# A 7x7 depthwise convolution on TensorE: from row bands to tiles of six by four pixels

## The chip, the cores and the metric

The kernel runs on one core of one Trainium2 chip. The metric is the device time of one execution in microseconds (us), median of the runs. A core has five engines that run side by side, each taking its own instructions in order: TensorE (PE; its weight loads are listed as PEld), VectorE (DVE), ScalarE (ACT), GpSimd (POOL) and SyncE (SP), whose queue here issues nearly all DMAs.

## The reference

Two attention layers on x of 4 images, 256 channels, 64 x 64 pixels, all in float32. Cut to what matters here, the second layer is:

```python
qkv = conv1x1(x, w_qkv, b_qkv)                 # 768 channels: q, k, v of 8 heads of 32
attn = softmax(q @ k.T * 32 ** -0.5)           # within each of 4 areas of 16 image rows
out = attn @ v
out = out + dwconv7(v, w_pe, b_pe)             # each channel its own 7x7 filter, padding 3
x = x + conv1x1(out, w_proj, b_proj)
```

The input of each layer is group-normalised. The first layer is attention of all 4096 pixels to 1024 keys that 2x2 convolutions with step 2 make. The change touches dwconv7 and what stands around it.

## The kernel before, in words

**Units.** The work is 128 units: batch by batch the first layer (A0 to A3), then the second (B0 to B3), 16 units each. A unit is 512 query pixels (a "chunk" of 8 image rows) and 128 channels (4 heads); it goes through 8 steps of 128 keys. In a step TensorE makes the scores of 4 heads (L261, tile s), ACT the exponentials (L265, tile p), TensorE the weighted sums (L272, tile av), and DVE adds up p (L797) for the divisors. The loop over steps at the end of the function writes all engines' orders out by hand: nothing is reordered later, so an engine whose next instruction waits keeps all behind it waiting.

**The plan.** All other work is put into this loop. `at(g, j, f)` has f emitted at unit g, step j; `task(n, f)` puts a generator into a side queue, of which one to three parts go on TensorE in each step. So projections, the convolution and their loads have fixed places among the steps of attention, and the places are the same constants before and after.

**v and the convolution.** `plan_values(b, c, start)` loads a chunk of the first layer's result (hv), normalises it on ACT (L243), makes v by matmuls (vals_ps) and copies it with its bias to the tile vout (L669), with zero columns at the sides (L658, L659). vout is stored twice: by four DMAs into vala for the attention of the second layer (L677), and by eight, one for each image row, into vals, the image with its rows in reverse order (L682). The starts are set so that batch 0 has 3.4 units per chunk, batch 1 1.0, batch 2 1.6 (the two overlap from unit 48 on) and batch 3 0.4 (units 66 to 70).

From unit 70.5, every 0.52 units, `plan_conv(n)` handles four channels of all batches. It loads from vals, for the upper and the lower half of the image, 42 rows three times, each time shifted by one column, so that 126 partitions hold (shift, row) (L705, tile rows). The 7x7 filter stands in a band matrix, loaded for 8 channels at a time (L717, tile band). For each channel and half three matmuls accumulate, for the columns 0, 3 and 6 of the filter and their neighbours (L732): 126 x 32 weights, 32 output rows, 4 batches x 64 columns = 256 moving columns. Four matmuls with 32 output partitions each stand side by side in the array. ACT copies the result (L739), and two DMAs store it in conv, channel by batch by pixel (L741).

`load_rest` reads a chunk back from conv by one DMA (L556, tile cv), `add_conv` adds the attention and the bias on DVE (L572), `project` multiplies by w_proj (tile ops), adds the residual (L583) and stores (L586). For batches 0 to 2 this runs from unit 105.3, one chunk each 0.8 units; for batch 3 beside its own attention.

**DMAs.** The SP queue issues all of these in the order of the plan. Each of its DMAs uses one of eight semaphores in rotation and so waits for the landing of the one eight before it.

Of the kernel before, what the change touches and what calls it, by code (L numbers as in the profile page):

```python
# [32 lines left out]
XP = WW + 8  # L33
BAND = HH // 2 + 2 * HALO
BROWS = 42
TC = 8
NTAP = 49
# [17 lines left out]
def direct_path(  # L55
# [32 lines left out]

    vals = dram.tile([HH + 2 * HALO + BROWS - BAND, C, B, XP], FP, name="vals")

    vala = [[dram.tile([4, HD, NH, 4, XP], FP, name=f"vala_{b}_{a}") for a in range(NAREA)] for b in range(B)]
    conv = dram.tile([C, B, N], FP, name="conv")

    bands = dram.tile([C // TC, 9, BROWS + HH // 2 - 1, TC], FP, name="bands")

# [368 lines left out]
    def plan_b(b, u):  # L464
# [13 lines left out]
        def make_k(a, qd, half):  # L478
            if qd == 0 and half == 0:
                kvs["k"] = k_tile(("B", b, a))  # L480
            k, ps = kvs["k"], ps_side(f"k1ps_{b}_{a}_{qd}_{half}")
            for t in range(CT):
                product(
                    ps, lhsT=wqkv_sb[:, t, 1, qd * P : (qd + 1) * P],
                    rhs=hs[a][:, t, half * CH : (half + 1) * CH], start=(t == 0), stop=(t == CT - 1),
                )
                if t == 0:
                    yield

            S.activation(  # L490
                k[:, qd, :].rearrange("p (j t i) -> p t j i", t=4, i=32)[:, 2 * half : 2 * half + 2],
                ps.rearrange("p (t j i) -> p t j i", t=2, i=32), AF.Identity, bias=bqkv_sb[:, 1, qd : qd + 1],
            )
            if qd == 1 and half == 1:
                ks["B", b, a] = k

        def load_v(a, half):
            vcs[a, half] = pool.tile([P, NH // 2, 4, XP], FP, tag="vc", name=f"vc_{b}_{a}_{half}", bufs=2)
            nc.sync.dma_start(
                vcs[a, half], vala[b][a][:, :, half * NH // 2 : (half + 1) * NH // 2].rearrange("t c h r x -> (t c) h r x")  # L500
            )

        def make_v(a, half):

            if half == 0:
                kvs["v"] = v_tile(("B", b, a))
            v, vc = kvs["v"], vcs.pop((a, half))
            V.transpose(
                out=v[:, :, half * P : (half + 1) * P].rearrange("p (r j) (h c) -> p h r j c", j=2, c=HD),
                in_=vc[:, :, :, HALO : HALO + WW].rearrange("p h r (j w) -> p h r j w", w=HD),  # L510
            )
            if half == 1:
                vs["B", b, a] = v
# [40 lines left out]
        def load_rest(c):  # L554
            cv = chunk_tile(f"cv_{b}_{c}")
            nc.sync.dma_start(cv, conv[:, b, c * CH : (c + 1) * CH].rearrange("(t p) n -> p t n", p=P))  # L556
            att = None
# [5 lines left out]
            rest[c] = cv, att  # L563

        def add_conv(c):
            cv, att = rest[c]
# [4 lines left out]
            for t in range(CT):  # L571
                V.scalar_tensor_tensor(cv[:, t, :], cv[:, t, :], bpe_sb[:, t : t + 1], att[:, t, :], ALU.add, ALU.add)  # L572

        def project(c, to):
# [7 lines left out]
            xm = made_x[c]  # L582
            V.scalar_tensor_tensor(xm[:, to, :], ps, bproj_sb[:, to : to + 1], xm[:, to, :], ALU.add, ALU.add)  # L583
            if to == 1:
# [29 lines left out]


    def plan_zeros(g):


        def zeros():
            zero = pool.tile([P, 8 * B * XP], FP, tag="rows", name="zero", bufs=2)  # L620
            V.memset(zero, 0.0)
            for lo, hi in ((0, 3), (67, 71), (71, 74)):
                nc.sync.dma_start(
                    vals[lo:hi].rearrange("r c b x -> (r c b x)").rearrange("(p n) -> p n", n=8 * B * XP),
                    zero[: (hi - lo) * C // 8],
                )
            flat = bands.rearrange("k x i c -> (k x i c)").rearrange("(p n) -> p n", p=P)
            nc.sync.dma_start(flat, zero[:, : flat.shape[1]])

        def taps():  # L630
            tap = pool.tile([NTAP, C], FP, tag="cout", name="tap", bufs=2)
            nc.sync.dma_start(tap, wpe.rearrange("c k -> k c"))
            for n in range(7):
                nc.sync.dma_start(
                    bands[:, :7, BAND - 1 - n, :].rearrange("k x c -> x k c"),
                    tap[7 * n : 7 * n + 7, :].rearrange("x (k c) -> x k c", c=TC),
                )
# [6 lines left out]
    def plan_values(b, c, start):  # L644
# [10 lines left out]
        def values(t):  # L655
            if t == 0:
                vout = made["v"] = pool.tile([P, CT, RC, XP], FP, tag="rows", name=f"vout_{b}_{c}", bufs=2)
                V.memset(vout[:, :, :, :HALO], 0.0)  # L658
                V.memset(vout[:, :, :, HALO + WW :], 0.0)  # L659
            h, vout = made["h"], made["v"]  # L660
            ps = ps_side(f"vals_ps_{b}_{c}_{t}")
            for tt in range(CT):
# [6 lines left out]
            S.activation(  # L669
                vout[:, t, :, HALO : HALO + WW], ps.rearrange("p (r w) -> p r w", w=WW), AF.Identity,  # L670
                bias=bqkv_sb[:, 2, t : t + 1],
            )
            if t == CT - 1:
                stored[b, c] = True
                for n in range(2):
                    for tt in range(CT):
                        nc.sync.dma_start(  # L677
                            vala[b][c // 2][2 * (c % 2) + n, :, 4 * tt : 4 * tt + 4].rearrange("c h r x -> h c (r x)"),
                            vout[:, tt, 4 * n : 4 * n + 4, :].rearrange("p r x -> p (r x)"),
                        )  # L680
                for r in range(RC):
                    nc.sync.dma_start(  # L682
                        vals[HALO + HH - 1 - c * RC - r, :, b, :].rearrange("(t p) x -> p t x", p=P), vout[:, :, r, :]
                    )

# [6 lines left out]

    band_tiles = {}

    def plan_conv(n, start):

        made = {}

        def load():
            row, size = C * B * XP, 4 * B * XP  # L700
            need(stored, (B - 1, NCH - 1))
            made["x"] = xs = pool.tile([3 * BROWS, 2, 4, B, XP], FP, tag="rows", name=f"rows_{n}", bufs=2)
            for half in range(2):
                for s in range(3):
                    nc.sync.dma_start(  # L705
                        xs[s * BROWS : (s + 1) * BROWS, half].rearrange("p c b x -> p (c b x)")[:, : size - s],
                        bass.AP(
                            tensor=vals.tensor, offset=vals.offset + (1 - half) * (HH // 2) * row + n * size + s,
                            ap=[[row, BROWS], [1, size - s]],
                        ),  # L710
                    )
            k, part = divmod(4 * n, TC)
            if part == 0:
                band = band_tiles[k] = pool.tile([3 * BROWS, 3, HH // 2, TC], FP, tag="band", name=f"band_{k}", bufs=2)
                step = (BROWS + HH // 2 - 1) * TC
                for s in range(3):
                    nc.sync.dma_start(  # L717
                        band[s * BROWS : (s + 1) * BROWS].rearrange("p g y c -> p g (y c)"),
                        bass.AP(
                            tensor=bands.tensor, offset=bands.offset + (9 * k + s) * step,  # L720
                            ap=[[TC, BROWS], [3 * step, 3], [1, HH // 2 * TC]],
                        ),
                    )

        def convolve():
            xs, (k, part) = made.pop("x"), divmod(4 * n, TC)
            ps = ps_side(f"conv_ps_{n}").rearrange("p (i b x) -> p i b x", i=2, b=B)
            for i in range(2):
                for g in range(3):
                    for m in range(4):  # L730
                        c = 2 * (m // 2) + i
                        T.matmul(  # L732
                            ps[HD * m : HD * m + HD, i], lhsT=band_tiles[k][:, g, :, part + c],
                            rhs=xs[:, m % 2, c, :, 3 * g : 3 * g + WW], start=(g == 0), stop=(g == 2),
                        )
                    if (i, g) in ((0, 1), (1, 0)):
                        yield
            out = pool.tile([P, 2 * B, WW], FP, tag="cout", name=f"cout_{n}", bufs=2)
            S.copy(out, ps.rearrange("p i b x -> p (i b) x"))  # L739
            for ch in range(2):  # L740
                nc.sync.dma_start(  # L741
                    conv[4 * n + 2 * ch : 4 * n + 2 * ch + 2].rearrange("i b (y x) -> y (i b) x", x=WW),
                    out[HH * ch : HH * (ch + 1)],
                )

        when = int(start * NKT)
        at(0, when, load)
        at(0, when + 4, lambda: task(3, convolve))


# [693 lines left out]
```

## Time and profile before

| | |
|---|---|
| median of 3 runs (lowest, highest) | 3271.41 us (3269.73, 3272.02) |
| profiled execution: its time, its span | 3270.47 us, 3268.7 us |
| TensorE clock granted | 0.997 |
| DMA packets, bytes, mean rate | 319853, 397.27 MB, 122 GB/s |
| under 512 B | 182652 packets |
| convolution, first to last matmul | 1797.9 to 2653.2 us |
| stores into vals, first to last issue | 542.6 to 1786.0 us |
| reads of conv, first to last issue | 2657.6 to 3211.8 us |

The span runs from the first to the last instruction; the profiled execution has its own time, which stands 0.9 us under the median. "Busy" is the time in which an engine has an instruction in work; a group is all instructions of one line, operation and tile. DMA issues of SP are listed with the time that the queue took to issue them, not to move the data.

### The profile page before, as it was taken

What the parts mean: (1) busy time and instruction counts of PE and PEld (TensorE: products, weight loads), DVE (VectorE), ACT (ScalarE), POOL (GpSimd) and SP (SyncE); (2) the same over time, 40 slices, a digit from 0 to 9 for tenths busy, and PEclk for the clock granted to TensorE, in tenths of its full rate; (3) what the DMA queues carried; (4) which work ended last, traced back from release to release, by engine and by line L of the source; (5) the groups of instructions that cost most, each with busy time, mean ns of one, the idle gap of its engine ahead of it and who ended that gap; (6) DMA issues with size and microseconds to landing.
All of it is one profiled execution on the core that took longest, in us unless ns stands there. A gap on an engine that the chain in (4) does not pass through costs nothing.

```text
span 3268.7 us, 72561 instructions
## 1 busy us (share of the span) xinstructions
PE 3218.2 (98%) x29730; PEld 961.1 (29%) x29730; DVE 2491.6 (76%) x2621; ACT 2525.6 (77%) x2993; POOL 487.2 (15%) x923
## 2 busy tenths in 40 slices
PE   7999999999999999999999999999999999999997
PEld 4233323333233322222222333333333322222221
DVE  3777897779877787778876767666776778888887
ACT  3888788887888888888887777777777787776765
POOL 0111121111211111111111111111111111111111
PEclk9999999999999999999999999999999999999999
DMA  5312212313322213553236667676766643445431
GB/s 179 80 64 73 77 66 90 100 59 116 100 69 84 65 63 91 148 138 113 82 120 158 162 151 178 159 174 141 180 171 153 172 142 123 166 147 172 155 121 57
DMA packets 319853, 397.27 MB, mean 122 GB/s; under 512 B 182652, under 2 KB 215708, under 8 KB 319192
## 3 DMA queue, kind: packets, MB, share of 16 engines
q1 hardware_dynamic: 291064, 356.06, 38.5%
q0 software_dynamic: 28448, 36.48, 4.2%
q8 instruction: 236, 3.87, 0.5%
q14 instruction: 105, 0.86, 0.1%
HBM read 285.98 MB, written 106.42 MB: 120 GB/s over the span
## 4 chain that ended last, share of the span: by engine, by line
PE 94%; DMA 2%; issue 1%; ACT 1%; DVE 1%; SPq 0%; POOL 0%; DVEq 0%; ACTq 0%; POOLq 0%
PE s L261 33%; PE av L272 29%; PE conv_ps L732 5%; PE den L281 4%; PE k0ps L155 3%; PE k1ps L155 3%; PE q1ps L155 3%; PE v0ps L155 3%; PE q0ps L155 3%; PE ops L155 3%; PE vals_ps L155 3%; ACT p L265 1%; DVE p L797 1%; DMA conv<-cout 0%; DMA rows<-vals 0%
## 5 line engine op out<-in xcount | busy, mean ns | idle before, releaser
L797 DVE TENSOR_TENSOR p<-p 128x1024 f32<-128x1024 f32 x1792 | 2113.3, 1219 | 623.1 <-ACT p L265 583.3
L265 ACT ACTIVATE p<-s 128x1024 f32<-128x1024 f32 x2048 | 2016.9, 1027 | 571.9 <-PE s L261 564.0
L261 PE MATMUL s<-q,k_A 32*128 32x512 f32 x4096 | 608.2, 640 | 1.4 <-ACT p L265 0.9
L261 PE MATMUL s<-q,k_B 32*128 32x512 f32 x4096 | 588.7, 640 | 1.1 <-ACT p L265 0.8
L272 PE MATMUL av<-p,v_A 128*32 128x512 f32 x4096 | 551.1, 603 | 0.0
L272 PE MATMUL av<-p,v_B 128*32 128x512 f32 x4096 | 546.0, 604 | 0.0
L308 POOL DMA_DIRECT2D rb<-recs x508 | 252.4, 502 | 454.1 <-DMA recs<-few 377.5
L306 POOL DMA_DIRECT2D recs<-few x127 | 70.2, 553 | 1423.2 <-DVE sums L305 1372.1
L261 PEld LDWEIGHTS s<-q,k_A 32*128 32x128 f32 x4096 | 176.3, 183 | 357.8 <-issue 273.3
L261 PEld LDWEIGHTS s<-q,k_B 32*128 32x128 f32 x4096 | 162.5, 182 | 363.3 <-issue 290.5
L272 PEld LDWEIGHTS av<-p,v_A 128*32 128x32 f32 x4096 | 89.4, 108 | 383.0 <-issue 335.0
L272 PEld LDWEIGHTS av<-p,v_B 128*32 128x32 f32 x4096 | 87.6, 108 | 378.8 <-issue 332.9
L732 PE MATMUL conv_ps<-rows,band 126*32 126x256 f32 x3072 | 195.1, 379 | 0.0
L732 PEld LDWEIGHTS conv_ps<-rows,band 126*32 126x32 f32 x3072 | 123.0, 139 | 113.0 <-issue 78.3
L297 POOL DMA_DIRECT2D rows<-den_sb x127 | 74.6, 587 | 433.3 <-ACT den_sb L290 424.1
L281 PE MATMUL den<-p,ones 128*32 128x512 f32 x1024 | 137.8, 605 | 0.4 <-DVE p L797 0.4
L155 PE MATMUL ops<-cv,wp_sb 128*32 128x512 f32 x1024 | 129.8, 600 | 6.0 <-issue 6.0
L155 PE MATMUL vals_ps<-hv,wqkv_sb 128*32 128x512 f32 x1024 | 130.1, 596 | 3.9 <-ACT vout L669 3.8
L155 PE MATMUL k0ps<-taps,wk_sb 128*32 128x256 f32 x2048 | 130.6, 383 | 3.0 <-ACT taps L243 3.0
L155 PE MATMUL k1ps<-h,wqkv_sb 128*32 128x512 f32 x1024 | 128.7, 593 | 2.4 <-ACT cout L739 1.6
L155 PE MATMUL q0ps<-hq,wq_sb 128*32 128x512 f32 x1024 | 129.8, 592 | 0.0
L155 PE MATMUL q1ps<-h,wqkv_sb 128*32 128x512 f32 x1024 | 129.7, 596 | 0.1
(87 smaller groups left out, 1594.9 us busy)
## 6 DMA issues: line engine op xcount, KB each, us to landing
rb<-recs POOLq DMA_DIRECT2D x508, 64.0 KB, 2.4
rows<-vals SPq DMA_DIRECT2D x128, 189.0 KB
rows<-vals SPq DMA_DIRECT2D x128, 188.8 KB
rows<-vals SPq DMA_DIRECT2D x128, 188.7 KB
vala<-vout SPq DMA_DIRECT2D x128, 144.0 KB
vals<-vout SPq DMA_DIRECT2D x256, 72.0 KB
vc<-vala SPq DMA_DIRECT2D x32, 576.0 KB
hq<-in_x SPq DMA_DIRECT2D x32, 512.0 KB
```

What stands on the lines that cost most here:

```text
L155: T.matmul(out[cols, :], lhsT=lhsT[:, cols], rhs=rhs, start=start, stop=stop)
L261: T.matmul(pairs[h // 2][:, h % 2, :], lhsT=k[rows, unit[0], j * P : (j + 1) * P], rhs=q[rows, :], start=True, stop=True,)
L265: exps = [lambda i=i: S.activation(p[i], pairs[i], AF.Exp, scale=SCALE) for i in range(2)]
L272: T.matmul(av[HD * h : HD * h + HD, :], lhsT=v[:, j, unit[0] * P + HD * h : unit[0] * P + HD * h + HD], rhs=p[h // 2][:, h % 2, :], start= ...
L281: T.matmul(dens[g][HD * h : HD * h + HD, :], lhsT=ones, rhs=p[h // 2][:, h % 2, :], start=True, stop=True,)
L297: G.dma_start(rows, den_sb[0:P:HD, :])
L306: G.dma_start(recs.rearrange("h (q n) -> (h q) n", n=CH // HD), few[:, 1, :])
L308: G.dma_start(rb[HD * h : HD * h + HD, :], recs[h : h + 1, :].to_broadcast([HD, CH]))
L732: T.matmul(ps[HD * m : HD * m + HD, i], lhsT=band_tiles[k][:, g, :, part + c], rhs=xs[:, m % 2, c, :, 3 * g : 3 * g + WW], start=(g == 0), ...
L797: soon(1, lambda i=i: V.tensor_add(ps[0][i], ps[0][i], ps[j][i]))
```

## The change

The image is cut into tiles of 6 rows by 4 columns (11 tiles down, the last row of tiles partly empty; 16 across). One output tile of one channel depends on 12 x 10 = 120 pixels of v. These 120 pixels stand in the partitions, the 24 outputs (in an array strip of 32 with 8 rows more that aren't used) in the weights' columns, and the tiles of all batches are the moving columns: one matmul, without accumulation, makes the convolution for 6 (or 5) rows of tiles x 4 batches x 16 tiles.

So that a partition's run in HBM is contiguous, vals is laid out by every fourth pixel of a row: row, column modulo 4, channel, batch, column divided by 4. vala is laid out by every fourth pixel too, and k, v and the results are reordered to go with it. conv becomes channel, pixel in the tile, tile row, batch, tile column.

- vals is stored by 32 DMAs per chunk (8 rows x 2 channel halves x 2), with runs of 18 values.
- The filter table is filled by 49 DMAs, one for each tap, in place of 7, and loaded for 16 channels by 10 DMAs in place of 8 by 3.
- rows is loaded for four channels in two halves (6 and 5 rows of tiles), four DMAs each, three halves ahead; the pool of rows and vout tiles has three buffers in place of two.
- There are 4 matmuls and one copy for each half; each half is stored by one DMA.
- conv is read back by 16 DMAs per chunk (8 rows x 2 channel halves), with runs of 16 values; cv is then ordered by column modulo 4, and the additions on DVE read and write it in that order.
- The copy of k with its bias is made in two halves.

```diff
@@ vals, conv
-    vals = dram.tile([HH + 2 * HALO + BROWS - BAND, C, B, XP], FP, name="vals")
+    vals = dram.tile([TY * NY + 2 * HALO, TX, C, B, XT], FP, name="vals")
-    conv = dram.tile([C, B, N], FP, name="conv")
+    conv = dram.tile([C, HD, NY, B, WW // TX], FP, name="conv")
@@ plan_values: stores of a chunk
                 for r in range(RC):
-                    nc.sync.dma_start(
-                        vals[HALO + HH - 1 - c * RC - r, :, b, :].rearrange("(t p) x -> p t x", p=P), vout[:, :, r, :]
-                    )
+                    for t in range(CT):
+                        row, out = vals[HALO + HH - 1 - c * RC - r, :, t * P : (t + 1) * P, b, :], vout[:, t, r]
+                        nc.sync.dma_start(row[:3].rearrange("f p x -> p f x"), out[:, 1:])
+                        nc.sync.dma_start(row[3], out.rearrange("p f x -> p (f x)")[:, 1 : 1 + XT])
@@ taps
-            for n in range(7):
+            for n in range(NTAP):
                 nc.sync.dma_start(
...
@@ plan_conv: rows
-            for half in range(2):
-                for s in range(3):
-                    nc.sync.dma_start(
-                        xs[s * BROWS : (s + 1) * BROWS, half].rearrange("p c b x -> p (c b x)")[:, : size - s],
...
+        for a, f, fs in ((0, 0, 4), (1, 0, 4), (2, 0, 1), (2, 1, 1)):
+            p = 12 * (4 * a + f)
+            nc.sync.dma_start(
+                xs[p : p + 12 * fs].rearrange("p y c b x -> p y (c b x)")[:, : hi - lo, : size - 2],
...
@@ convolve
-            for i in range(2):
-                for g in range(3):
-                    for m in range(4):
-                        c = 2 * (m // 2) + i
-                        T.matmul(
-                            ps[HD * m : HD * m + HD, i], lhsT=band_tiles[k][:, g, :, part + c],
-                            rhs=xs[:, m % 2, c, :, 3 * g : 3 * g + WW], start=(g == 0), stop=(g == 2),
-                        )
+        for m in range(4):
+            T.matmul(
+                ps[HD * m : HD * m + HD].rearrange("p (y b x) -> p y b x", b=B, x=WW // TX),
+                lhsT=band_tiles[k].rearrange("p y (x c) -> p (y x) c", c=TC)[:, :, part + m],
+                rhs=xs[:, : hi - lo, m, :, : WW // TX], start=True, stop=True,
+            )
@@ load_rest
-            nc.sync.dma_start(cv, conv[:, b, c * CH : (c + 1) * CH].rearrange("(t p) n -> p t n", p=P))
+            for y in range(c * RC, (c + 1) * RC):
+                n, r = divmod(HH - 1 - y, TY)
+                r = TY - 1 - r
+                for t in range(CT):
+                    nc.sync.dma_start(
+                        cv[:, t, :].rearrange("p (f r x) -> p r f x", f=TX, r=RC)[:, y - c * RC],
+                        conv[t * P : (t + 1) * P, r * TX : (r + 1) * TX, n, b, :],
+                    )
@@ add_conv, project
+                V.scalar_tensor_tensor(
+                    by_column(cv[:, t, :]), by_column(cv[:, t, :]), bpe_sb[:, t : t + 1],
+                    att[:, t, :].rearrange("p (q f) -> p q f", f=TX), ALU.add, ALU.add,
+                )
...
+            x_to = xm[:, to, :].rearrange("p (q f) -> p q f", f=TX)
+            V.scalar_tensor_tensor(x_to, by_column(ps), bproj_sb[:, to : to + 1], x_to, ALU.add, ALU.add)
```

## The prediction

> **What bounds the kernel now.** I read the busy table first, then the chain that ended last, then the groups, then 100 us stretches.
>
> ```profile
> PE 3218.2 (98%) x29730; PEld 961.1 (29%) x29730; DVE 2491.6 (76%) x2621; ACT 2525.6 (77%) x2993; POOL 487.2 (15%) x923
> ...
> PE 94%; DMA 2%; issue 1%; ACT 1%; DVE 1%; SPq 0%; POOL 0%; DVEq 0%; ACTq 0%; POOLq 0%
> ...
> L732 PE MATMUL conv_ps<-rows,band 126*32 126x256 f32 x3072 | 195.1, 379 | 0.0
> ...
> L155 PE MATMUL k0ps<-taps,wk_sb 128*32 128x256 f32 x2048 | 130.6, 383 | 3.0 <-ACT taps L243 3.0
> ```
>
> TensorE is busy 98% and makes 94% of the chain, so time taken off it anywhere comes off the span, as long as nothing else ends later; the convolution is 195.1 us of it. The stretches show where:
>
> ```profile
> 1400.00:1500.00 100.00, 100.00 (x816) 25.32 (x812) 78.58 (x88) 86.74 (x105) 15.91 (x30) 1.00 0.51 142
> ...
> 1900.00:2000.00 100.00, 99.77 (x1020) 34.05 (x1016) 69.49 (x68) 74.53 (x87) 14.09 (x27) 1.00 0.68 164
> ...
> 2800.00:2900.00 100.00, 100.00 (x832) 25.19 (x828) 83.66 (x91) 73.42 (x83) 14.76 (x28) 1.00 0.44 150
> ```
>
> (Columns: PE, PEld, DVE, ACT, POOL busy, clock, DMA share, GB/s.) Three stages matter: the values stages (stores of v, up to 1786 us), the convolution (1798 to 2653) and the projections after it. TensorE is full in all three. So each stall that the change brings in one of them is added in full, and only the middle one gets shorter.
>
> The queue that is nowhere in that table is SP's, which issues every load and store of activations, in order. Its timeline at the end of the values stage (start, duration, line, DMA), and then the view of the tensor vals (least, median and longest issue in ns; who waited for it, us and times):
>
> ```profile
> 1762.09 3.15 SPq L677 DMA_DIRECT2D vala<-vout  x4
> 1765.28 8.69 SPq L682 DMA_DIRECT2D vals<-vout  x8
> 1774.02 1.22 SPq L471 DMA_DIRECT2D h<-xmid  x2
> 1775.36 3.80 SPq L677 DMA_DIRECT2D vala<-vout  x4
> 1779.20 7.14 SPq L682 DMA_DIRECT2D vals<-vout  x8
> 1786.38 1.01 SPq L705 DMA_DIRECT2D rows<-vals  x1
> ```
>
> ```profile
> L705 SPq DMA_DIRECT2D rows<-vals x384: 306/384/1669, 1786.4 to 2635.2; - x192
> L682 SPq DMA_DIRECT2D vals<-vout x256: 359/615/2145, 542.6 to 1786.0; - x128
> ...
>   PEld conv_ps L732: 0.3, 1
> ```
>
> The stores of one chunk of v (4 vala, 8 vals) take 11 us of SP back to back (1775.36 to 1786.34), the last chunk's end at 1786.3, the first rows load follows at once, and the first convolution matmul starts at 1797.9 with one wait of 0.3 us for its rows: no slack here. TensorE takes its instructions in order, so attention stands behind a late first convolution.
>
> [...] 126 rows 379 ns, 128 rows 383 ns, both 256 columns. [...] each vala store (outermost 4) brings 5 semaphore updates[...], and vala stores land 1.6 us apart, vals 0.34. [...] In this trace's packet records a 288 B packet takes 23.6 ns on average and a 256 B one 20.2, against 97.7 for 2 KB[...]. [...] the conv weights at a 32 B step: 139 ns per load against 110.
>
> **The change, part by part.**
>
> *Matmuls.* Four columns of tiles at a time, the moving columns per four channels fall from 2 x 3 x 256 = 1536 to 384 + 320 = 704, weights stay 32 wide. 195.1 x 704/1536 = 89.4 us: **105.7 us off TensorE**, all in the convolution stage. Weight loads (123 us for 3072, 1024 of them after, so 41 us, possibly more at the 64 B step) lie under the matmuls before them; uncovered they would cost that. Runs of 16 elements in the moving operand: unseen; I take 0 (high end 10 us). In that stage ACT goes from 75 to about 89% and DVE from 70 to 80% of a unit 12% shorter; neither becomes the bound.
>
> *Stores of v.* Per chunk 32 vals stores replace 8; vala is unchanged. SP: 32 chunks x 24 = 768 more DMAs. Each DMA waits for the one eight before it (eight semaphores in rotation); 8 in flight at the 2.3 us from issue to landing of the last vals store is no bound. Price of an issue: the present form (256 runs) took 467 to 470 ns back to back when nothing blocked it; a simple one (rows) 384. The two new forms are 384 and 128 runs; I take 0.47 and 0.385, with 0.04 between: 0.467 us each. The first eight stores still stand behind vala's four engines, as now: 10.5 us (median of the back-to-back chunks), less 1.3 for a shorter tail of 8 stores ahead (8 x 0.34 against about 8 x 0.18). Then 24 x 0.467 = 11.2. **20.4 us of SP per chunk** against 10.5. Packets of 72 B: between 13 ns (128 B in the trace) and 24; a pair of stores puts 34 on an engine, 0.4 to 0.8 us, under its 0.93 us of issue. Engine time doesn't bind.
>
> Where chunks come faster than that, SP falls behind. Two places, from the times of the vout copies:
> - Batches 1 and 2 overlap: chunks 10 to 19 are ready from 1301 to 1435. SP needs 10 x 20.4 + 16 other DMAs x 0.45 = 211 us, ends at 1512 instead of 1451.3: 61 us behind. Queued behind are loads that ACT normalises: hv issued at 1355.1 and used at 1362.1, hq at 1356.9 and 1374.6, hv at 1381.4 and 1393.3; after 4 to 5 us of landing they have 3, 13 and 7 us, say 9 with a few us of buffering. **Stall 52 us**: ACT waits in order, exps behind it, TensorE behind them.
> - Batch 3: eight chunks from 1680.8. 8 x 20.4 + 9 x 0.45 = 167, end at 1848 instead of 1786.3. **Stall 62 us**, at the first convolution or earlier through the three vout buffers, not twice.
> Single chunks elsewhere lag by 5 to 8 us, within slack: 0.
>
> *Rows, bands, taps.* Per four channels 8 + 2.5 + 2 DMAs instead of 6 + 1.5 + 2, some 5.5 of 13 us of SP: hidden under the other channels' matmuls, since loads go out three half-steps ahead; without that lead each half would wait some 4 us for its rows (landing median 4.7 us now). Taps: 42 more DMAs x 0.40 = 17 us of SP at about 153 us, before the first xc; that has about 13 us before its add and DVE has slack: 5 us.
>
> *Reading conv back.* Per chunk 16 DMAs of 512 runs (64 B) for one: 16 x 0.6 = 9.6 us more SP. Chunks were loaded about 27 us before their add (issued 2855.35, added 2882.5), so mostly hidden; xm, vc and h loads queue behind. 0 to 30, I take 10 us.
>
> *Strided operands.* k copy in two halves: some 0.2 us x 64 = 13 us on ACT, under its 20% of idle time: 0, 13 us if ACT were the bound. Column-order adds (L572, L583) 744 and 749 ns x 128: nothing, up to double; doubled they add 96 us to a DVE that idles about 90 us between 2690 and 3255. I take 0, high end 40.
>
> *Sum*, against the profiled 3270.5 us (span 3268.7): -105.7 + 52 + 62 + 5 + 10 = +23, 3294. The median of the runs is 0.9 above: **3295 us**.
>
> **Rivals.**
> - *SP is cheaper, and it is faster.* At S us per chunk the two stalls are (10S + 7 - 150 - 9) + (8S + 4 - 105.5); with the other 15 us they equal the 105.7 saved at S = 19.1, that is 0.41 us per short store. The shortest rows issues took 0.306; at 0.30 S is 16.4 and the time 3271 + 18 x (16.4 - 19.1) = 3222. For: those short issues. Against: they came after waits; back to back it was 0.384.
> - *The buffers absorb the lag*, and nearly all of TensorE's saving is seen: 3180. For: three vout buffers for two, DVE and ACT idle 20%. Against: the 0.3 us wait at the first convolution, TensorE in order.
> - *Short stores block one another*: each takes the 0.727 us that the stores of batch 3 average now. S = 10.5 - 1.3 + 24 x 0.77 = 27.7, 3271 + 18 x 8.6 = 3426. For: single stores up to 2.1 us. Against: those stood behind vala.
> - *DVE bounds the projections* (strided adds doubled): 3295 + 40 = 3335.
>
> **How the numbers follow.** Forecast 0.43 (own range 3255 to 3340), cheaper SP 0.27, absorbed 0.08, blocking 0.13, DVE 0.09. About 0.2% is what a measurement of this kernel tells from no change. Faster 0.27 + 0.08 and 0.01 of the forecast's low edge: 0.36; same 0.04; slower 0.60. The range 3205 to 3400 takes in the cheaper SP and the DVE case, and leaves out the absorbed one and most of the blocking one.
>
> **What would show it.** conv_ps matmuls near 89 us; vals stores x1024, SP taking about 20 us for a chunk back to back; the last vals store some 60 us later relative to the last vout copy; TensorE under 90% busy in the two values stretches, waits of ACT on hv or hq, and one of tens of us before the first conv_ps. Wrong if SP needs under 19 us per chunk, if the waits fall on idle time, or if the projections lose TensorE time.

## The result and the profile after

| | before | after |
|---|---|---|
| median of four runs (lowest, highest) | 3270.57 us (3268.65, 3272.02) | 3642.54 us (3641.67, 3648.39) |
| ratio, with its 95% interval | | 1.114 (1.112 to 1.116) |
| profiled span | 3268.7 us | 3640.9 us |
| span less TensorE's busy time | 50.5 us | 408.0 us |
| TensorE clock granted | 0.997 | 0.944 |
| DMA packets; of these under 512 B | 319853; 182652 | 815227; 613515 |

The change costs 372 us. Slower was the forecast, but by 24 us. The page of the profile after:

```profile
PE 3232.9 (89%) x27682; PEld 891.0 (24%) x27682; DVE 2511.6 (69%) x2621; ACT 2547.6 (70%) x3121; POOL 489.4 (13%) x923
...
PEclk9999999999999997878998799999999999999999
DMA  4122223233323134445424488787887775766662
...
PE 62%; DMA 17%; SPq 10%; issue 5%; DVE 3%; ACT 3%; POOL 0%; DVEq 0%; ACTq 0%; POOLq 0%
...
L757 PE MATMUL conv_ps<-rows,band 120*32 120x384 f32 (+1 forms) x1024 | 110.3, 503 | 126.9 <-DMA band<-bands 60.7
```

TensorE had 94% of the chain and has 62%. DMA and SP's queue, which were 2% and 0%, have 27%. The clock row has dips to 7 and 8 in the slices where TensorE is least busy. The convolution's matmuls are cheaper (110.3 us for 195.1), and 126.9 us of idle time now stand before them, where there was none. The stretches (PE, PEld, DVE, ACT, POOL busy, clock, DMA share, GB/s):

```profile
1400.00:1500.00 100.00, 48.20 (x348) 11.14 (x344) 31.96 (x37) 37.79 (x47) 6.85 (x13) 0.73 0.41 74
1500.00:1600.00 100.00, 63.15 (x468) 15.11 (x460) 42.84 (x49) 47.06 (x57) 7.95 (x15) 0.80 0.45 80
2230.00:2330.00 100.00, 90.64 (x756) 24.07 (x752) 68.86 (x68) 76.06 (x97) 14.19 (x27) 0.96 0.78 179
3100.00:3200.00 100.00, 99.40 (x824) 24.90 (x816) 87.76 (x90) 73.29 (x86) 14.79 (x28) 1.00 0.68 151
```

In the first two, the overlap of batches 1 and 2, no engine is full: TensorE 48 and 63%, ACT and DVE under 50%, the DMA engines 41 and 45%. What works is the queue that has no column here. SP's timeline has one of batch 3's chunks, its 4 vala and 32 vals stores (start, duration, line, DMA):

```profile
1991.56 2.60 SPq L699 DMA_DIRECT2D vala<-vout  x4
1994.20 0.55 SPq L707 DMA_DIRECT2D vals<-vout  x1
...
1999.12 0.39 SPq L707 DMA_DIRECT2D vals<-vout  x1
2000.94 0.32 SPq L708 DMA_DIRECT2D vals<-vout  x1
...
2003.40 1.82 SPq L707 DMA_DIRECT2D vals<-vout  x1
2005.26 0.62 SPq L708 DMA_DIRECT2D vals<-vout  x1
...
2007.17 0.43 SPq L707 DMA_DIRECT2D vals<-vout  x1
2007.65 0.48 SPq L708 DMA_DIRECT2D vals<-vout  x1
```

Most issues take 0.43 or 0.48 us, but some take 1 to 2, and between 1999.5 and 2000.9 SP stands, that is, it waits and issues nothing: that store waits for semaphore 107, the one of the vala store issued at 1993.31, which lands at 2000.92. The next chunk starts at 2015.8, 24 us after this one. In the overlap (1361 to 1650 us) SP's ten chunks take 289 us from the first issue to the last; it is issuing for 207 of them and stands some 39 of the rest for stores of v that haven't landed, so the issues are most of it, and the landings some. Who waits, from the view of waits (us in total, times, longest):

```profile
ACT hv L245 <- DMA hv<-xmid: 135.7, 10, 34.1
...
PE s L263 <- ACT p L267: 115.3, 12, 32.0
...
PE conv_ps L757 <- DMA band<-bands: 60.7, 5, 43.1
PE conv_ps L757 <- DMA rows<-vals: 55.1, 23, 6.2
...
DVE vout L680 <- DMA vals<-vout: 53.0, 5, 19.3
```

ACT waits for chunks whose loads stand behind stores, its exponentials come late behind that, and TensorE behind them. Then the first convolution waits (43.1), and later ones for rows and bands. By stage, from the first score matmul of the first unit named to that of the last one (us; the last two columns are experiments below):

| units | what is in them | before | after | v8_long | few_dmas |
|---|---|---|---|---|---|
| 2 to 5 | taps | 71.6 | 89.3 | 88.6 | 71.6 |
| 18 to 48 | v of batch 0 | 726.8 | 746.3 | 726.8 | 726.8 |
| 50 to 65 | v of batches 1 and 2 | 363.9 | 532.8 | 363.2 | 363.4 |
| 66 to 72 | v of batch 3, first convolution | 161.8 | 262.7 | 165.4 | 164.6 |
| 73 to 105 | convolution | 827.1 | 857.0 | 860.9 | 826.4 |
| 105 to 125 | projections | 513.3 | 550.5 | 551.2 | 518.5 |

The other units differ by under 3 us. Another view of the sum: idle time of TensorE rose by 357 us (408.0 - 50.5); busy time rose by 15, although the convolution's fell by 85. Most of that difference is the clock. In both traces it stands at full or at half speed and nowhere between; it goes to half 42 times after the change and 4 times before. TensorE is busy at half speed for 185.6 us after and 10.1 before; half of that, an estimate of what the clock costs, is 93 us after and 5 before (108 and 5 if it is estimated from the mean clock of stretches of 20 us). So idle +357, clock +88 to +103, and the convolution -94 at full clock (few_once below): 351 to 366 of the 372.

### The profile page after: what moved, and what is told of

Same layout as the page of the kernel before. It is cut to its first block, busy times and chain, and to the rows that moved or that the text cites. A ratio compares the mean times of both kernels' runs of the same rounds, so it can differ in the third digit from the quotient of the medians.

```text
span 3640.9 us, 70531 instructions
## 1 busy us (share of the span) xinstructions
PE 3232.9 (89%) x27682; PEld 891.0 (24%) x27682; DVE 2511.6 (69%) x2621; ACT 2547.6 (70%) x3121; POOL 489.4 (13%) x923
## 2 busy tenths in 40 slices
DMA packets 815227, 416.45 MB, mean 114 GB/s; under 512 B 613515, under 2 KB 735467, under 8 KB 814887
## 4 chain that ended last, share of the span: by engine, by line
PE 62%; DMA 17%; SPq 10%; issue 5%; DVE 3%; ACT 3%; POOL 0%; DVEq 0%; ACTq 0%; POOLq 0%
PE s L263 22%; PE av L274 19%; DMA vals<-vout 6%; DMA rows<-vals 6%; PE den L283 3%; PE v0ps L157 3%; PE k0ps L157 3%; PE q1ps L157 3%; SPq L708 2%; PE q0ps L157 2%; PE ops L157 2%; PE k1ps L157 2%; SPq L707 2%; ACT p L267 2%; SPq L564 2%
## 5 line engine op out<-in xcount | busy, mean ns | idle before, releaser
L263 PE MATMUL s<-q,k_A 32*128 32x512 f32 x4096 | 627.5, 651 | 105.1 <-ACT p L267 104.6
L263 PE MATMUL s<-q,k_B 32*128 32x512 f32 x4096 | 612.1, 660 | 11.0 <-ACT p L267 10.7
L274 PE MATMUL av<-p,v_A 128*32 128x512 f32 x4096 | 565.5, 615 | 0.0
L274 PE MATMUL av<-p,v_B 128*32 128x512 f32 x4096 | 553.4, 610 | 0.0
L757 PE MATMUL conv_ps<-rows,band 120*32 120x384 f32 (+1 forms) x1024 | 110.3, 503 | 126.9 <-DMA band<-bands 60.7
L157 PE MATMUL vals_ps<-hv,wqkv_sb 128*32 128x512 f32 x1024 | 138.3, 630 | 41.0 <-ACT vout L691 41.0
L157 PE MATMUL ops<-cv,wp_sb 128*32 128x512 f32 x1024 | 134.2, 619 | 30.0 <-DVE xm L602 23.6
L245 ACT ACTIVATE hv<-hv,norm_B 128x512 f32<-128x512 f32 x64 | 52.1, 816 | 151.5 <-DMA hv<-xmid 135.7
L283 PE MATMUL den<-p,ones 128*32 128x512 f32 x1024 | 146.1, 620 | 12.3 <-DVE p L827 12.3
L763 ACT COPY cout<-conv_ps 128x384 f32<-128x384 f32 (+1 forms) x128 | 59.3, 464 | 122.3 <-PE conv_ps L757 84.8
L157 PE MATMUL k0ps<-taps,wk_sb 128*32 128x256 f32 x2048 | 130.6, 383 | 3.0 <-ACT taps L245 3.0
```

The costliest lines, as they stand in the source:

```text
L157: T.matmul(out[cols, :], lhsT=lhsT[:, cols], rhs=rhs, start=start, stop=stop)
L263: T.matmul(pairs[h // 2][:, h % 2, :], lhsT=k[rows, unit[0], j * P : (j + 1) * P], rhs=q[rows, :], start=True, stop=True,)
L274: T.matmul(av[HD * h : HD * h + HD, :], lhsT=v[:, j, unit[0] * P + HD * h : unit[0] * P + HD * h + HD], rhs=p[h // 2][:, h % 2, :], start= ...
L283: T.matmul(dens[g][HD * h : HD * h + HD, :], lhsT=ones, rhs=p[h // 2][:, h % 2, :], start=True, stop=True,)
L757: T.matmul(ps[HD * m : HD * m + HD].rearrange("p (y b x) -> p y b x", b=B, x=WW // TX), lhsT=band_tiles[k].rearrange("p y (x c) -> p (y x) ...
```

## The experiments

Theory of the stores: SP issues v's stores more slowly than chunks come, and all of the loss in units 18 to 72 is theirs. Its first rival: the DMA engines can't take that many short runs. For the convolution's stage the question was why nothing of the saving shows. Each of these is one run with a profile; before took 3268.7 to 3271.1 us beside them. The four runs of the changed kernel above differ by up to 7 us, so differences of a few us between single runs say nothing.

**v8_long.** The order in HBM is another one (a channel's four columns side by side), so the convolution reads other data.

```diff
-                    for t in range(CT):
...
-                        nc.sync.dma_start(row[:3].rearrange("f p x -> p f x"), out[:, 1:])
-                        nc.sync.dma_start(row[3], out.rearrange("p f x -> p (f x)")[:, 1 : 1 + XT])
...
+                        bass.AP(tensor=vals.tensor, offset=at_row, ap=[[TX * XT, P], [P * TX * XT, CT], [1, TX * XT]]),
+                        vout[:, :, r].rearrange("p t f x -> p t (f x)"),
```

For a row, two stores of [128, 3, 18] and [128, 18] per channel half become one of [128, 2, 72] for both, with runs of 288 B.

> The changed kernel with the stores of v into vals as before in number and form: 8 DMAs per chunk, 256 runs of 288 B each, put one after another into the same rows of vals. So the convolution reads the right amount of data by the same pattern, but in another order (its results are not those of the reference). Theory 'issue' (SP's in-order queue is behind because of the number of DMAs, and ACT, DVE and TensorE wait for loads queued behind them): units 5 to 72, 1906 us in the changed kernel, return to about 1620 us as before, the time to about 3355 us. Theory 'packets' (the runs of 72 B are what the DMA engines are slow at): the same, 3355 us. This run gives the size of what both speak of.

3362.3 us. Every values stage is back within 4 us of its time before, and the others keep what they lost (table). Its stretches, to hold against those above:

```profile
1400.00:1500.00 100.00, 100.00 (x816) 25.45 (x808) 78.46 (x87) 86.67 (x105) 14.74 (x28) 1.00 0.58 161
1500.00:1600.00 100.00, 99.99 (x808) 25.35 (x800) 81.62 (x89) 85.52 (x103) 15.27 (x29) 1.00 0.33 96
```

So 280 of the 372 us are these stores. Four kernels ask what it is about them: the number of DMAs, or of runs. In each the order in HBM is another one, except where said.

**v32_mid.** `for s in range(2)`: stores of [128, 36], 32 DMAs, 144 B.

> The changed kernel with 32 stores of v per chunk, but each of 128 runs of 144 B, half as many runs in all (4096 per chunk for 8192), in another order in vals (results are not those of the reference). Theory 'issue': as many DMAs, so nearly all of the loss stays: 3600 to 3640 us, units 5 to 72 about 1870 to 1900 us. Theory 'packets': half of the runs are gone, so about half of the 290 us: 3500 us.

**v8_short.** Stores of [128, 8, 18] for two rows, the partitions' runs 72 B apart.

> The changed kernel with 8 stores of v per chunk, each of 1024 runs of 72 B: as many short runs as in the changed kernel, a quarter of the DMAs (another order in vals, results are not those of the reference). Theory 'issue': the loss goes but for some us: 3355 to 3390 us, units 5 to 72 within 40 us of before (1616). Theory 'packets': the loss stays, 3600 us or more.

**v8_true.** The same, but with the channels' runs 288 B apart, as the changed kernel has them.

> The stores of v in 8 DMAs of 1024 runs of 72 B per chunk instead of 32 of 384 and 128, at the addresses of the changed kernel (runs of neighbouring channels 288 B apart, so that v is laid out as there but for the fourth column's shift, which is left out). Theory 'number of DMAs': SP's service of a chunk falls to that of the kernel before (10 to 13 us), the two values stages (units 50 to 72) return to 526 us from 795, and the run takes about 3365 us. Theory 'short runs': 8192 runs cost what they cost in the first try with adjacent runs (39 ns on a DMA engine), the stages stay above 740 us, and the run takes 3580 us or more.

**v32_long.** Stores of [64, 72]: half of the channels of a half, 288 B.

> The stores of v in 32 DMAs per chunk as in the changed kernel, but each of 64 runs of 288 B (2048 runs per chunk, as many as before the change; the order of v in HBM is another). Theory 'number of DMAs': 32 issues of about 0.37 us and 4 of 0.53 with 0.04 between are 15 us of SP per chunk, 4 to 5 more than before; the values stages (units 50 to 72) lose 60 to 110 us and the run takes 3420 to 3470. Theory 'number of runs': nothing is lost there and the run takes 3355 to 3375.

| | DMAs x runs, bytes | time, us | units 50 to 65 | 66 to 72 | SP per chunk, us: vals + vala + standing |
|---|---|---|---|---|---|
| before | 8 x 256, 288 | 3270 | 363.9 | 161.8 | 11.1: 6.2 + 2.5 + 2.4 |
| v8_long | 8 x 256, 288 | 3362.3 | 363.2 | 165.4 | 11.0: 6.6 + 2.5 + 2.0 |
| after | 16 x 384 and 16 x 128, 72 | 3642.5 | 532.8 | 262.7 | 23.8: 18.0 + 2.6 + 3.2 |
| v32_mid | 32 x 128, 144 | 3582.6 | 473.3 | 256.6 | 23.1: 15.6 + 2.8 + 4.7 |
| v32_long | 32 x 64, 288 | 3670.6 | 526.3 | 284.3 | 26.5: 20.2 + 2.5 + 3.8 |
| v8_true | 8 x 1024, 72 | 3597.0 | 519.7 | 234.3 | 19.3: 15.1 + 3.7 + 0.6 |
| v8_short | 8 x 1024, 72 | 3635.4 | 503.7 | 264.5 | 22.2: 16.1 + 5.3 + 0.9 |

(SP per chunk: mean of the last seven chunks of batch 3, which follow one another with hardly a pause. Standing includes some 0.04 us between two issues: 1.6 us of a chunk of 36 DMAs, 0.5 of one of 12.) v32_mid comes near the time that the number of DMAs would give (17 us under its range), v8_short and v8_true fall in the range that the number of runs would give, so neither theory holds alone; v32_long misses both, by 200 us and more. With the number of runs of before, its 32 DMAs are dearer than after:

```profile
L707 SPq DMA_DIRECT2D vals<-vout x1024: 445/595/2475, 559.2 to 2106.6; - x171
```

A store of 64 partitions takes SP 0.595 us (median), one of 128 partitions with 128 or 384 runs 0.43 to 0.48; so an edit meant to leave only the number made each of them dearer as well, and its time says that the number suffices, not what it costs alone. On the other side, 8 DMAs with the changed kernel's runs (v8_true) gain only 46 us. There the DMA engines are nearly full:

```profile
1400.00:1500.00 100.00, 57.26 (x412) 13.59 (x416) 37.88 (x43) 47.09 (x58) 5.55 (x11) 0.76 0.79 89
1500.00:1600.00 100.00, 67.92 (x512) 16.39 (x508) 45.12 (x49) 53.20 (x65) 9.78 (x19) 0.81 0.90 75
```

The DMA share, 0.41 and 0.45 after, is 0.79 and 0.90 here: packets of 72 B take 25.5 ns on average in v8_true, 11.7 after, and SP's issues lengthen to 1.86 us (median; the shortest take 0.58). That fits engines that don't take the packets as fast as SP offers them; no run shows it by itself. In v8_short neighbouring channels' runs touch, and their packets take 38.8 ns. So the theory of the stores stands, and "number or length" was a false choice: with either one put back and the other kept, the vals stores still take 15 us or more of SP per chunk. By SP's times and the DMA share the changed kernel is at the first limit, with the second close behind.

**h_pool.** Does the lag reach TensorE through the loads behind the stores? `nc.sync` becomes `nc.gpsimd` for the loads of hv and hq; nothing is left out.

> The changed kernel with the loads of the chunks that are normalised for v and for queries (hv and hq, 32 each of two kinds) on GpSimd's queue; the stores stay on SP. Theory 'loads behind stores in SP's order': the waits of ACT on hv and hq (136 us on hv) go, the stage of units 50 to 65 falls from 533 to 400 to 470 us, with DVE waiting for a free vout in their place where SP is still 50 us or more behind; the run takes 3540 to 3600. If the lag comes through buffers and the DMA engines anyway, the stage stays at 510 or more and the run above 3615.

3618.2 us, 3 above the limit of the second theory; units 50 to 65 take 494.8, between the two. The wait on hv is gone, and waits for vout take its place: DVE 103.2 and ACT 95.4 us (53.0 and 20.5 after), until TensorE's vals_ps waits 82.7. So the order in the queue is worth 38 of the 169 us; the waits that took its place say that the rest is the lag itself, which three vout buffers don't hold.

**vals_pool.** The same question the other way round: all 32 stores on GpSimd's queue; nothing is left out.

> The changed kernel with all 32 stores of v issued on GpSimd's queue instead of SP's. Theory 'SP in order' (the time is lost because loads and other stores stand behind the stores of v): the waits of the overlap of batches 1 and 2 and of batch 0's chunks go nearly all, the stage of units 50 to 65 falls from 533 to under 420, and only batch 3's stay, since the first convolution needs all of v; the run takes 3450 to 3530. Theory 'the DMA engines are the limit' (short runs hold up all other transfers): 50 to 65 stays above 480 and the run above 3580. GpSimd's own work (the reciprocals of attention) comes late if its issues are dear: then both stages can be worse.

3780.5 us, with 585.1 in units 50 to 65: above what both theories were about, so the run doesn't decide between them. The doubt at the end of the expectation came true.

```profile
DVE att_A L313 <- DMA rb<-recs: 225.3, 16, 36.7
...
PE den L283 <- DVE p L827: 177.1, 21, 24.9
```

POOL's busy time goes from 489.4 to 1151.4 us, 0.65 us for each of the 1024 stores; before these stores it also stands, 95 us for earlier ones to land and 53 for vout (ACT's copies). Attention's divisors stand behind all this. Of POOL's time the issues, 670 us (385.3 + 285.2), are the larger part.

**band1, rows1, cv_one.** One kind of the change's other pieces each. band1: one load of 120 partitions for ten. rows1: one load of 120 partitions for four, runs of 6.9 KB. Both bring other data of the same size. cv_one: one DMA of [128, 2, 512] for 16 (conv in another order).

> The band of conv weights comes by one DMA over 120 partitions instead of ten (the weights of a tile then lie in another order of columns). Theory 'SP in the convolution': the waits that come at every fourth group of channels, behind 8.4 us of band issues, go: TensorE idle on conv_ps falls from 82 to under 30 us after the first one, the stage of units 73 to 105 from 857 to 800 or less, and the run takes 3585 us or less. Theory 'rows loads' (bytes and packets of the rows set the pace): the stage keeps 840 us or more and the run takes 3620 or more.

> The rows of a half come by one DMA over 120 partitions with one run of 6.9 or 5.8 KB each instead of four DMAs with runs of 1.1 KB (other data, the same bytes within 1%). Theory 'SP in the convolution': three issues fewer per half, 1.2 us of some 13 per half; the bursts of band issues remain, so the stage of units 73 to 105 falls by 10 to 30 us from 857 and the run takes 3610 to 3635. Theory 'rows loads' by packets: the stage falls to 780 or less, the run to 3565 or less.

> The changed kernel with each chunk of conv read back by one DMA of 256 runs of 2 KB in place of 16 with 512 runs of 64 B each (the pixels come in another order, results are not those of the reference). Theory 'issue': units 105 to 125 go from 550 to about 515 us as before, the time to about 3605 us. Rival: in that stretch DVE's additions in column order cost the time (they stay): 550 us stay, 3640 us.

band1 3592.5, rows1 3594.0, cv_one 3616.8 us. band1 takes units 73 to 105 from 857.0 to 822.1, between its two expectations; rows1 takes them to 821.2 and so beats the expectation of the first theory, but reaches nowhere near the second's. So each of the two kinds of load makes up a part of the delay. cv_one takes units 105 to 125 from 550.5 to 518.6, so the additions in column order, its rival, cost little. Here is one of the bursts that band1 removes, with what waits for it, in the changed kernel's timeline:

```profile
2308.37 0.90 PE L757 MATMUL conv_ps<-rows,band 120*32 120x384 f32 x8
...
2310.63 8.36 SPq L742 DMA_DIRECT2D band<-bands  x10
...
2320.70 1.52 PE L757 MATMUL conv_ps<-rows,band 120*32 120x384 f32 x8 [6.66 <-DMA band<-bands]
```

There is such a burst at every fourth group of channels. Its first eight issues, to every fourth partition, take 0.76 us each (median), the last two, to contiguous partitions, 0.53 and 0.37. And the same matmuls take 1.52 us after the wait, 0.90 without: the clock is at half from 2318.5 to 2325.3 us.

**few_dmas.** All pieces together: v8_long, cv_one, band1, and the taps in 7. The matmuls are the changed kernel's.

> All four kinds of loads and stores that the change had cut into pieces are made with few DMAs again: v in 8 with 288 B runs, conv read back in 1, band in 1, taps in 7 (the orders in HBM are other ones); the matmuls and their operands on chip are the changed kernel's. If the pieces are the whole cause, TensorE's 105.7 us come off the time before, with some idle time and clock lost: 3165 to 3200 us. If the convolution stage is bound by the rows (27% more bytes) or by strided operands, it stays near 3260 to 3300.

3276.4 us: the second expectation. With the pieces gone, taps, values and projections are back (table), and yet the 106 us aren't seen: the convolution's stage takes 826.4.

```profile
2200.00:2300.00 100.00, 91.79 (x768) 24.35 (x760) 70.34 (x69) 77.40 (x99) 13.52 (x26) 0.97 0.82 184
```

```profile
L750 PE MATMUL conv_ps<-rows,band 120*32 120x384 f32 (+1 forms) x1024 | 106.4, 486 | 61.3 <-DMA rows<-vals 38.3
```

```profile
PE conv_ps L750 <- DMA rows<-vals: 38.3, 19, 3.9
...
PE conv_ps L750 <- DMA band<-bands: 14.9, 4, 5.0
```

The median of the time from one half to the next is 5.5 us, but a quarter follow by 2.7 us or less; a half brings 0.82 or 0.69 MB (6 or 5 x 120 runs of 1144 B), by estimate some 4 us at the 176 to 195 GB/s moved in this stage. If so, three halves ahead are no lead in a burst. Three kernels on top of few_dmas:

```diff
-        for a, f, fs in ((0, 0, 4), (1, 0, 4), (2, 0, 1), (2, 1, 1)):
+        for a, f, fs in ((0, 0, 4), (1, 0, 4), (2, 0, 1), (2, 1, 1)) if n == 0 else ():
```

**few_once** (above; later groups use the first tiles again):

> The kernel with few DMAs (v in 8, conv read back in 1, band in 1, taps in 7), and of the rows loads only those of the first four channels: all later convolution matmuls read these two tiles again. Theory 'rows loads arrive too late in bursts' (halves follow one another by 2.6 us, a half's rows take some 4 us of the DMA engines): without them the waits on conv_ps go (62 us in the kernel with few DMAs), the clock stays at 1.00, the stage of units 73 to 105 takes 827 - 89 = 740 us, and the run takes 3180 to 3195 us. Theory 'something else bounds the stage' (ACT, DVE, strided operands): it stays above 800 us and the run above 3250.

**few_rows1** (the rows of rows1):

> The kernel with few DMAs, and the rows of a half by one DMA with one run of 6.9 or 5.8 KB per partition (other data, the same bytes within 1%). If the time that packets take on the DMA engines makes the rows late, the stage of units 73 to 105 falls from 826 to 770 or less and the run takes 3220 or less; if the bytes or the landing after issue do, it stays within 15 us of 3276.

**few_spread** (`yield` after two of the four matmuls, `task(2, convolve, ...)`):

> The kernel with few DMAs, and each half of a convolution group split over two steps (two matmuls, then two), so that halves follow one another at some 5 us in a burst instead of 2.6. Theory 'rows late in bursts': idle time on conv_ps falls from 62 to under 20 us and the run takes 3230 or less. Other theories: 3265 to 3290.

few_once 3184.9, few_rows1 3230.1, few_spread 3243.1 us; their stages 740.8, 785.1, 796.7. few_once's stage is within a microsecond of the first theory's 740, and its stretches and groups are what the prediction had in mind:

```profile
2000.00:2100.00 100.00, 100.00 (x860) 27.59 (x856) 78.33 (x77) 85.51 (x110) 15.89 (x30) 1.00 0.25 80
2300.00:2400.00 100.00, 100.00 (x864) 27.11 (x856) 77.41 (x76) 85.53 (x109) 15.90 (x30) 1.00 0.25 80
```

```profile
L753 PE MATMUL conv_ps<-rows,band 120*32 120x384 f32 x512 | 54.1, 491 | 1.2 <-issue 1.2
L753 PE MATMUL conv_ps<-rows,band 120*32 120x320 f32 x512 | 47.0, 438 | 0.6 <-DMA rows<-vals 0.6
```

So the saving is real, and the rows' loads take it back: shown by taking them away, with their issues, packets and bytes. few_rows1 gives 46 us of it back, by longer runs and fewer issues; it stays short of the time expected, and half of the idle time stays. few_spread gives 33 back and misses its time too, but for a reason of its own:

```profile
L750 PE MATMUL conv_ps<-rows,band 120*32 120x384 f32 (+1 forms) x1024 | 131.4, 471 | 18.9 <-DMA rows<-vals 15.2
```

The idle time before the convolution fell from 61.3 to 18.9 us, as the theory of the bursts said (under 20). But the convolution's busy time rose from 106.4 to 131.4: two matmuls side by side in a step of their own take 0.77 us, all four in one step 0.83, so the edit itself cost 25 us. And it spread less than was meant: only 38 of the 128 halves have their two pairs in two steps, since a fuller side queue puts both parts into one. A longer lead wasn't tried.

**mix.** A version with nothing left out: 24 stores of v per chunk, v of batch 1 earlier and of batch 3 wider apart, the band two DMAs at a time, halves over two steps, taps over seven units.

```diff
+                        nc.sync.dma_start(row[:3, t].rearrange("f p x -> p f x"), vout[:, t, r, 1:])
...
-            plan_values(b, c, ends[b] + 1.8 + (14.5 if b == 1 else 0) + (3.4, 1.0, 1.6, 0.4)[b] * c)
+            plan_values(b, c, ends[b] + 1.8 + (9.0 if b == 1 else 0) + (3.2, 1.0, 1.6, 0.7)[b] * c)
```

> Nothing is left out. The changed kernel with 24 stores of v per chunk for 32 (the fourth column of both channel halves in one), chunks of batch 1 begun 5.5 units earlier and those of batch 3 spaced by 0.7 units for 0.4, the convolution begun 1.5 units later, the band loaded two DMAs at a time ahead of its use, each half of a group over two steps, and the taps' stores spread over seven units. If spreading hides SP's work: values stages lose 20 to 60 us instead of 270, the convolution stage takes about 800, taps nothing, reading conv back 27: 3270 to 3310 us. If SP's lag doesn't depend on the spacing: 3450 or more.

3472.3 us: 170 less than the changed kernel, 202 more than before: the second expectation's number, though hardly its reason: with the wider spacing and fewer stores, units 66 to 73 lose 43 us (99 in the changed kernel). Taps cost nothing, reading conv back still costs 41 (554.3 in units 105 to 125), and the convolution's stage takes 780.9, 46 less than before:

```profile
1400.00:1500.00 100.00, 71.96 (x520) 17.52 (x512) 54.33 (x59) 58.44 (x69) 11.05 (x21) 0.85 0.55 80
...
2230.00:2330.00 100.00, 99.03 (x828) 27.63 (x828) 73.96 (x72) 82.89 (x106) 14.74 (x28) 1.00 0.90 200
```

But a chunk of v still takes 20.5 us of SP in batch 3 and 19 to 32 elsewhere, up to 17 of them standing, for ACT's copy of the second half of vout and for earlier vals stores to land. Between the chunks of batch 1 there is one unit (some 23 us), so the lag starts earlier: units 18 to 50 take 849.7 (770.5 before), 50 to 65 440.0. As mix changes several things at once, it doesn't show what each is worth. No version with the convolution's true data was found that beats before; by these figures it would take a way to write v in fewer and longer runs, and none was tried that keeps the data.

## Why the prediction was wrong, step by step

The forecast had the right parts, TensorE's saving against SP's lag, and failed above all at two of its steps. That rows and bands are hidden: the convolution's stage was to gain 105.7 us and lost 29.9, an error of 136. And the size of the two stalls, 114 us together: the two stages lost 270, an error of 156.

- *Matmuls, -105.7 us.* Right, a little large. In the kernel before, busy time goes with the moving columns (1024 matmuls of 512 columns take 129.8 us, q0ps; 2048 of 256 columns 126.2 and 130.6, v0ps and k0ps), and the forecast scaled by them alone. But with all data at hand (few_once) they take 101.1 us for the 89.4 forecast, 94.0 less than 195.1. Per moving column the larger form costs 0.281 ns for 0.248, so columns alone don't set it; strided operands and weight loads may have a part, which wasn't separated.
- *SP's 20.4 us per chunk.* Failed, the first mis-sized term: 23.8 in batch 3, 26.6 in the overlap. The issue prices were near (medians 0.433 for 0.47, 0.484 for 0.385). But the first 12 DMAs take 10.8 us in batch 3, where the forecast took 1.3 off the 10.5 for a shorter tail, and the other 24 take 0.545 each, gaps included, for 0.467: the medians alone are 0.46 and the gaps 0.04, and some issues take 1 to 2 us. In the overlap it is 12.2 us and 0.60 each: there SP also waits for earlier vals stores to land, 23 us over the ten chunks, which "8 in flight" had put at nothing.
- *Stalls of 52 and 62 us.* Mechanism right, sizes wrong. Batch 3's stores end 98.6 us later relative to their start (204.2 for 105.6), and its stage lost 101. In the overlap the ten chunks took 288.8 us of SP for 150.3, 138.5 more, where the sum had 61, and the stage lost 169. With the measured service the same sums give 266 + 7 - 150 - 9 = 114 and 199 + 4 - 105.5 = 97: batch 3 is settled, and half of the overlap's error is the term before. Another 15 are the other loads and pauses between chunks, 22.5 us where the sum had 7. Some 40 are left. Of the stage's 532.8 us TensorE is idle 141 and busy 391.7, 28 more than the whole stage took before, and the half clock alone takes 29 there: that would fill most of them, but no run separates them.
- *No price for idle time.* The step that wasn't there. In the trace of the changed kernel TensorE has 35 idle stretches of over 3 us, and in each of them, or at most 1.2 us after it, the clock goes to half or is there already; 40 of the 42 spells at half have at least 2 us of idle time in the 4 us before them. The eight matmuls after the wait of 6.66 us take 1.52 us for 0.90, and the granted clock is 0.73 in the worst stretch. The slower clock comes on top of the stalls, by the estimate above 88 to 103 us in all, about a quarter of the loss.
- *Rows and bands hidden.* Failed, the largest single error: the stage was to gain 105.7 and lost 30. The argument took means (5.5 of 13 us of SP per four channels); the halves come in bursts, eight of the band's ten issues are dearer (0.76 for 0.4), and the rows bring 96.6 MB for 74.3, with packets that take 7387 us over all engines for some 4900 (an estimate: the packets of 4600 to 4608 B took 5798 before, but 4096 of them are loads of vc), in a stage that was to be an eighth shorter.
- *Single chunks, 0.* Failed: 19.5 us in units 18 to 48, gone with v8_long. *Taps, 5*: 17.7, gone with few_dmas. *Reading conv back, 10*: 37, 32 of it gone with cv_one.
- *Strided operands.* L587 on DVE takes 1.13 us for 0.745, L602 0.748 for 0.749: 25 us of DVE, inside the range given. They cost at most 5: few_dmas has them, and its projections take 518.5 for 513.3.
- *The rivals.* "Short stores block one another" was nearest in its mechanism, S = 27.7 for 24 to 27 measured. Its time, 3426, failed by the terms that it shared with the forecast: convolution's gain, clock, taps, conv. The rival of a cheaper SP left out the 0.04 us between issues that the forecast has: with 0.306 + 0.04, S is 17.5 and its time 3242.
- *Short packets.* Per byte a packet of 288 B took 1.7 times as long as one of 2 KB in the figures of the prediction (23.6 and 97.7 ns), and one of 72 B after the change 3.4 times (11.7 ns). So short runs do cost engine time; no run shows by what mechanism.

## What to carry to other kernels

A layout that cuts rows into short runs must be priced on the queue that issues it, with its tail and the waits of its semaphores, at the pace at which the work comes at its fastest, and not by single issues and means; look for the stretch with the shortest spacing. Shorter work in one stage is a gain only if its data comes as early as the new pace asks: when a step's matmuls are halved, the next rows have half the time to land. And TensorE's stalls were paid twice here, as idle time (357 us) and as slow matmuls after it (88 to 103, an estimate).

## What the runs showed of the hardware

- SP's issue price went by form more than by runs: 0.43 us for [128, 36] (128 runs) and for [128, 3, 18] (384 runs) alike, 0.484 for [128, 18], 0.595 for [64, 72], 0.53 and 0.37 for 12 contiguous partitions, 0.76 for 12 at a step of four. Stores of 1024 runs took at least 0.58, in the median 1.86.
- A 72 B packet took 11.7 ns in 32 DMAs per chunk, 25.5 in 8, and 38.8 where the channels' runs touch. How much of this is waiting at full engines, and why touching runs are dearer, stays open.
- The vala stores held up the vals stores behind them. Of the chunk shown above, the vala stores land 1.8 us apart, the last at 2000.92, each with four semaphore updates (a fifth comes within 0.5 us of the issue's end) where a vals store brings 16. The vals store issued at 1994.20 has twelve of its updates by 1998.18 and the last four from 2000.85 to 2001.43; it and those behind it land from 2001.43 on, 0.2 to 0.4 us apart. That a vala store uses four of the 16 engines is an estimate from these updates.
- In the traces of before and after TensorE's clock was at full or at half speed and nowhere between: 42 spells at half, 406 us in all, in the changed kernel, and 4, 24 us in all, before. In few_once, with 1.8 us of idle time before the convolution's matmuls, the granted clock was 0.997.
